# Keys and queries of a chunk made together as a 2 by 2 block product with seven products, the queries kept in DRAM

## The chip, the core and the metric

The kernel runs on one core of a Trainium2 chip. The metric is device time in microseconds (us). The kernel before took a median of 2603.17 us over three runs (2600.44 to 2604.17). Engines are named as the profile names them: PE (TensorE matmuls; PEld are its weight loads), DVE (VectorE), ACT (ScalarE), POOL (GpSimd) and SP (the queue that issues nearly all DMAs). All data is float32.

## The reference

Two layers run on x of shape 4 x 512 x 64 x 64 (four images, 512 channels, 4096 pixels). The first is self-attention over the pixels of an image:

```
q = wq @ xf + bq;  k = wk @ xf + bk;  v = wv @ xf + bv     # (4, 128, 4096)
attn = softmax(q^T k)                                      # (4, 4096, 4096)
x1 = wo @ (v attn^T) + bo + x
```

The second is an involution block: `out = relu(W1 x1)`, a 49-tap (7 x 7) weight per pixel and group made from `out`, the weighted sum of the 49 shifted copies of `out`, then `W3` and the residual x1.

## The kernel before

**Stages.** An image is worked on in 8 chunks of 512 pixels (`CH`). For each of the four images `b`, a **keys stage** (`keys_values`) makes all keys and values, then an **attention stage** (`attention`) goes through the 8 query chunks. In the keys stage the chunks come in the order 2, 3, ..., 7, 1, 0; a chunk gives `pk` (4 matmuls of 512 columns) for the keys, and `pv` (16 matmuls of 128 columns) for the values. ACT moves both out of PSUM. In the attention stage each of 32 steps of a chunk makes one score tile `pss` (keys by queries), its exponential `pt` on ACT, one matmul into `po`, and on DVE a running sum `pacc` of the `pt` tiles. At step 24 of a chunk `queries` makes the queries of the next chunk: four matmuls of 512 columns into `pq`, moved out by ACT. The queries of chunk 0 are made in the keys stage.

**Work beside it.** A finished chunk goes through `finish_block` (normalising, `pwo` and the residual on DVE at L565, `p` for W1) and its result is written to DRAM (`pix`), from where windows come back into a ring in SBUF. The involution runs on units of 4 image rows, 16 of them per image: DVE multiplies a piece of the ring by the tap weights (`prod`, L358), POOL adds the product to `acc` (L382, folded at L391), DVE transposes the sum (`turned`, L406), and `close_chunk` applies W3 (`py`, residual on DVE at L463). 49 taps make a unit; a "tap row" below is one tap of one unit.

**What sets the order.** The work of the involution and of the finishing is spread between the matmuls by hand: `chores()` is called after a few matmuls, and runs steps of the generators `finishing`, `closing` and `taps`. A planner holds a clock of PE's time (`pe`, advanced by `mm`) and the times at which DVE, POOL and the DMAs would be free (`takes`). A tap is only issued when DVE's planned backlog is at most 3.5 us (4.5 for the last image) and POOL's is at most `lag`. Behind this the tile layer puts each engine's instructions into an order of its own; an engine runs that order strictly. After the last attention stage a tail runs what is left of the involution. PSUM pools: `ps_s` (two banks, for `pk` and `pss`), `ps1` (single banks `po`, `acc`, and the tap weights), `ps` (two banks, the rest). The x tiles come from six buffers, the `pt` tiles from five.

Of the kernel before, what the change touches and what calls it, by code (L numbers as in the profile page):

```python
# [8 lines left out]
F32 = mybir.dt.float32  # L9
# [58 lines left out]

PE_COLUMN = 0.43 / 256
DVE_OP, POOL_OP = 0.7, 1.28  # L70
DVE_TAPS, POOL_TAPS = (0.16, 0.27), (0.19, 0.55)
ROW_US, X_US, PIX_US, LAND_US = 2.2, 3.8, 1.5, 3.0
HOP_US = 0.8
# [12 lines left out]
def fast_path(  # L86
# [22 lines left out]
    def pool(name, bufs, **kw):  # L109
# [35 lines left out]
    okr = const.tile([P, 1], F32, name="okr")  # L145


    turns = [
        scratch.tile([CH // P, P, P], F32, tag=f"turns{i}", name=f"turns{i}") for i in range(2)
    ]  # L150
# [13 lines left out]
    reds, sums_c = {}, {}  # L164
    written = {}
    landing = {}
    lag = 0.0
    low, load = 0, 0

    def until(us):  # L170
# [14 lines left out]
        nc.sync.dma_start(xs[b, c], x_r[b, :, :, c * CH : (c + 1) * CH])  # L185


    for cols in (slice(0, P), slice(P, O_WV)):
        nc.scalar.dma_start(wt[:, cols], wts[:, cols])
    nc.scalar.dma_start(vec, vecs)  # L190
    c0, c1 = KEYS[:2]
    xs = {(0, c0): xpool.tile([P, CT, CH], F32, tag="x", name=f"x_0_{c0}")}
    for t in range(CT):
        nc.sync.dma_start(xs[0, c0][:, t, :], x_r[0, :, t, c0 * CH : (c0 + 1) * CH])
    nc.sync.dma_start(wt[:, O_WV:O_WQ], wts[:, O_WV:O_WQ])
    load_x(0, c1)
    nc.sync.dma_start(wt[:, O_WQ:], wts[:, O_WQ:O_WR])
    nc.vector.memset(ones, 1.0)

    warm = ps.tile([P, P], F32, tag="mm", name="warm")  # L200
# [16 lines left out]
    def v1(i):  # L217
        return vec[:, i : i + 1]
# [89 lines left out]
    def involution():  # L308
        nonlocal low, due
        while True:  # L310
# [15 lines left out]
            for o, (x, dy, n) in enumerate(ops):  # L326
                if o and dy >= DYS[1][0] > ops[o - 1][1]:
                    low = base + UR
                    pump()
                    if tail and units:  # L330
                        early[units[0]] = weights(*units[0])
                rows = [(base + dy + t * 2) % RING for t in range(NT)]
                while base + dy + n + NT > load:
                    yield "wait"
                landed = max(landing[base + dy + i] for i in range(n + NT))
                while not tail and (
                    pe < max(begin, landed)
                    or free["dve"] > pe + (4.5 if b == B - 1 else 3.5)
                    or free["pool"] > pe + lag
                ):  # L340
                    yield "wait"
                free["pool"] = max(free["pool"], takes("dve", DVE_TAPS[0] + DVE_TAPS[1] * n))
                takes("pool", POOL_TAPS[0] + POOL_TAPS[1] * n)
                due -= n
                d0 = dy - DYS[dy >= DYS[1][0]][0]
                first = x == 0 and dy < DYS[1][0]
                prod, p0 = acc, d0
                if not first:
                    prod, p0 = prods.tile(
                        [P, NT, 4, P], F32, tag="prod", name=f"prod_{b}_{u}_{o}"  # L350
                    ), 0
                col = (x * K + dy) * G
                lines = ring[:, rows[0] : rows[0] + n, x, :]
                image = bass.AP(
                    tensor=lines.tensor, offset=lines.offset,
                    ap=[lines.ap[0], [(rows[1] - rows[0]) * K * P, NT], [K * P, n], [1, P]],
                )
                product = nc.vector.tensor_tensor(  # L358
                    prod[:, :, p0 : p0 + n, :].rearrange("p t d (g c) -> p t d g c", g=G),
                    image.rearrange("p t d (g c) -> p t d g c", g=G),  # L360
                    pw[:, :, col : col + n * G].unsqueeze(3)
                    .broadcast_to([P, NT, n * G, GC])
                    .rearrange("p t (d g) c -> p t d g c", d=n),
                    ALU.mult,
                )
                if not tail:
                    tc.keep_in_program_order(product)
                if first:
                    pass
                elif tail and o % 2:  # L370

                    begun = pa is not None
                    if not begun:
                        pa = ps1.tile([P, NT, P], F32, tag=("po", "acc")[u % 2], name=f"pa_{b}_{u}")
                    for t in range(NT):
                        for d in range(n):
                            mm(
                                pa[:, t, :], prod[:, t, d, :], ident,
                                not begun and t == d == 0, False,
                            )  # L380
                else:
                    nc.gpsimd.tensor_tensor(  # L382
                        acc[:, :, d0 : d0 + n, :], acc[:, :, d0 : d0 + n, :], prod[:, :, :n, :],
                        ALU.add,
                    )
                yield
# [85 lines left out]
            nc.sync.dma_start(out_r[b, :, :, c * CH + off : c * CH + off + n], xt)  # L472


    def keys_values(b):
        kt = kvpool.tile([P, N], F32, tag="k", name=f"k_{b}")
        vT = kvpool.tile([P, N // P, P], F32, tag="v", name=f"v_{b}")

        for i, c in enumerate(KEYS):
            for k in KEYS[i + 1 : i + 3]:  # L480
                if (b, k) not in xs:
                    load_x(b, k)
            if c == 0:

                q = queries(b, 0, 0, CH)
            if b < 2 and i == 4:
                for rows in (slice(0, PAD), slice(PAD + H, None)):
                    nc.sync.dma_start(pix[b][rows].rearrange("r w c -> w r c"), zero)
                for cols in (slice(0, PAD), slice(PAD + W, None)):
                    nc.sync.dma_start(pix[b][PAD : PAD + H, cols, :], zero[:H])  # L490
            xt = xs[b, c] if c < KEEP else xs.pop((b, c))
            pk = ps_s.tile([P, CH], F32, tag="s", name=f"pk_{b}_{c}")
            for t in range(CT):
                mm(pk, w_slice(O_WK, t), xt[:, t, :], t == 0, t == CT - 1)
                if t % 2:
                    chores()
            nc.scalar.activation(
                kt[:, c * CH : (c + 1) * CH], pk, AF.Identity, bias=v1(V_BK)
            )
            pv = ps1.tile([P, 4, P], F32, tag=("po", "acc")[i % 2], name=f"pv_{b}_{c}")  # L500
            for j in range(4):
                for t in range(CT):
                    mm(
                        pv[:, j, :], xt[:, t, j * P : (j + 1) * P], w_slice(O_WV, t),
                        t == 0, t == CT - 1,
                    )
                if j % 2:
                    chores()
            nc.scalar.copy(vT[:, 4 * c : 4 * c + 4, :], pv)
        return kt, vT, q  # L510

    def queries(b, c, off, n):
        xt = xs[b, c][:, :, off : off + n]
        pq = ps.tile([P, CH], F32, tag="mm", name=f"pq_{b}_{c}_{off}")[:, :n]
        for t in range(CT):
            mm(pq, w_slice(O_WQ, t), xt[:, t, :], t == 0, t == CT - 1)
        q = work2.tile([P, CH], F32, tag="q", name=f"q_{b}_{c}_{off}")[:, :n]
        nc.scalar.activation(q, pq, AF.Identity, bias=v1(V_BQ))
        return q


# [198 lines left out]

    taps = [involution()]
    for b in range(B):
        lag = POOL_LAG[0]
        kv = keys_values(b)
        lag = POOL_LAG[1]
        if b == 0:

            pb = ps.tile([P, CT], F32, tag="mm", name="pb")
# [429 lines left out]
```

## Time and profile before

| | us |
|---|---|
| median of three runs | 2603.17 |
| the profiled execution, its own time | 2601.34 |
| span of the profiled execution | 2599.4 |
| PE busy / DVE busy / POOL busy / ACT busy | 2583.8 / 1874.6 / 1831.2 / 835.9 |
| keys stage of the second image (first to last matmul of it) | 616.64 to 689.55 |
| start of the last sum of the `pt` tiles (L715) | 2530.3 |

The granted PE clock is 1.000. In the lists of groups, a line gives the source line, engine, operation, tiles, sizes and count, then the busy time and the mean length of one in ns, then idle time of the engine just before it with what ended it. A float32 matmul shows as two PE instructions, so 128 matmuls of `pk` are 256 instructions. The end of a matmul in the trace is modelled, so the distance from start to start is the better measure of what it costs. In the timeline a line has its start in us, its length, engine, line and operation, and in brackets the idle time before it.

### The profile page before, as it was taken

How to read it: one execution, taken by the hardware profiler on the slowest of the kernel's cores; microseconds unless marked ns; L12 is line 12 of the kernel's file. 1: busy time of each engine (PE TensorE's matmuls, PEld its weight loads, DVE VectorE, ACT ScalarE, POOL GpSimd, SP SyncE). 2: the span in 40 equal slices, each digit the busy share in tenths (PEclk: the TensorE clock that was granted, in tenths of full speed). 3: DMA queues.
4: the chain of work that ended last, by engine and by line, in shares of the span. 5: the costliest groups of instructions: out<-in, count | busy, mean ns of one | idle time of the engine just before them, and what ended most of it. 6: DMA issues, size and time to landing. Idle time of an engine off the chain costs nothing. (4 is left out here: it accounts for less than half of the span.)

```text
span 2599.4 us, 24518 instructions
## 1 busy us (share of the span) xinstructions
PE 2583.8 (99%) x7462; PEld 1242.4 (48%) x7462; DVE 1874.6 (72%) x2679; ACT 835.9 (32%) x1379; POOL 1831.2 (70%) x1202
## 2 busy tenths in 40 slices
PE   9999999999999999999999999999999999999998
PEld 7444444445544444444654444444464444444577
DVE  0347778877575787788676677788856677777888
ACT  1333333332233333333223333333323333333330
POOL 0006788877881788888885468887877577778986
PEclk9999999999999999999999999999999999999999
DMA  6033233445615343233651434434463432223243
GB/s 237 1 74 63 55 81 78 99 99 150 164 43 113 63 101 87 66 83 80 182 134 44 105 69 101 97 83 85 109 175 79 113 94 73 71 63 75 66 112 92
DMA packets 208797, 244.32 MB, mean 94 GB/s; under 512 B 109640, under 2 KB 128528, under 8 KB 208528
## 3 DMA queue, kind: packets, MB, share of 16 engines
q1 hardware_dynamic: 208224, 242.31, 38.7%
q8 instruction: 60, 0.98, 0.2%
q14 instruction: 81, 0.66, 0.1%
q10 hardware_dynamic: 432, 0.36, 0.0%
HBM read 193.57 MB, written 49.06 MB: 93 GB/s over the span
## 5 line engine op out<-in xcount | busy, mean ns | idle before, releaser
L382 POOL TENSOR_TENSOR acc<-acc,prod 128x768 f32<-128x768 f32 (+3 forms) x1066 | 1707.1, 1620 | 746.0 <-DVE prod L358 701.9
L222 PE MATMUL pss<-q,k 128*128 128x512 f32 (+1 forms) x2112 | 1055.7, 584 | 0.0
L222 PE MATMUL po<-pt,v 128*128 128x512 f32 (+1 forms) x2112 | 1047.2, 580 | 0.0
L681 ACT ACTIVATE pt<-pss 128x512 f32<-128x512 f32 x1024 | 611.3, 597 | 1242.5 <-PE pss L222 1158.4
L358 DVE TENSOR_TENSOR prod<-ring,pw 128x512 f32<-128x512 f32 (+3 forms) x1092 | 888.5, 849 | 47.2 <-POOL acc L382 44.2
L712 DVE TENSOR_TENSOR pacc<-pacc,pt 128x512 f32<-128x512 f32 x958 | 666.0, 695 | 236.9 <-ACT pt L681 209.5
L222 PEld LDWEIGHTS po<-pt,v 128*128 128x128 f32 x2112 | 398.8, 190 | 480.9 <-issue 460.4
L222 PEld LDWEIGHTS pss<-q,k 128*128 128x128 f32 x2112 | 391.5, 190 | 466.8 <-issue 462.0
L406 DVE STREAM_TRANSPOSE turned<-acc 128x256 f32<-128x256 f32 x48 | 21.4, 445 | 218.4 <-POOL acc L391 218.4
L222 PE MATMUL py<-accT,wt 128*128 128x512 f32 (+1 forms) x264 | 132.2, 584 | 4.1 <-DVE x L463 3.5
L222 PE MATMUL pwo<-on,wt 128*128 128x512 f32 (+1 forms) x264 | 128.5, 579 | 0.0
L391 POOL TENSOR_TENSOR acc<-acc 128x512 f32<-128x512 f32 x122 | 121.6, 997 | 9.6
L222 PEld LDWEIGHTS pv<-wt,x 128*128 128x128 f32 x1024 | 119.6, 192 | 15.3 <-issue 15.3
L463 DVE SCALAR_TENSOR_TENSOR x<-py,vec,x 128x512 f32<-128x512 f32 (+1 forms) x132 | 95.9, 727 | 38.3 <-PE py L222 38.0
L222 PE MATMUL pv<-wt,x 128*128 128x128 f32 x1024 | 120.2, 275 | 0.0
L222 PE MATMUL p<-x,wt 128*128 128x512 f32 (+1 forms) x264 | 119.3, 580 | 0.0
L222 PE MATMUL pk<-x,wt 128*128 128x512 f32 x256 | 117.7, 599 | 0.0
L592 ACT ACTIVATE x<-x,vec 128x512 f32<-128x512 f32 (+1 forms) x132 | 92.9, 706 | 74.9 <-PE p L222 58.1
L222 PE MATMUL pq<-x,wt 128*128 128x512 f32 (+1 forms) x264 | 115.3, 579 | 0.0
L565 DVE SCALAR_TENSOR_TENSOR x<-pwo,bo,x 128x512 f32<-128x512 f32 (+1 forms) x132 | 95.3, 728 | 21.2 <-PE pwo L222 19.9
L358 DVE TENSOR_TENSOR acc<-ring,pw 128x1024 f32<-128x1024 f32 (+1 forms) x84 | 78.7, 956 | 15.6 <-PE pw L222 15.6
L222 PEld LDWEIGHTS pq<-x,wt 128*128 128x128 f32 x264 | 50.1, 190 | 59.7 <-issue 56.4
(69 smaller groups left out, 727.5 us busy)
## 6 DMA issues: line engine op xcount, KB each, us to landing
x<-x_dram SPq DMA_DIRECT2D x55, 1024.0 KB, 5.5
ring<-pix SPq DMA_DIRECT2D x74, 448.0 KB, 7.0
ring<-pix SPq DMA_DIRECT2D x24, 1344.0 KB, 9.7
out_dram<-x SPq DMA_DIRECT2D x31, 1024.0 KB, 4.6
ring<-pix SPq DMA_DIRECT2D x24, 896.0 KB, 10.5
ring<-pix SPq DMA_DIRECT2D x30, 672.0 KB, 10.8
ring<-pix SPq DMA_DIRECT2D x6, 2240.0 KB, 19.6
pix<-o1t SPq DMA_DIRECT2D x192, 32.0 KB, 1.7
```

The source lines that it names most:

```text
L222: return nc.tensor.matmul(o, lhsT=lhsT, rhs=rhs, start=start, stop=stop)
L358: product = nc.vector.tensor_tensor(prod[:, :, p0 : p0 + n, :].rearrange("p t d (g c) -> p t d g c", g=G), image.rearrange("p t d (g c) -> ...
L382: nc.gpsimd.tensor_tensor(acc[:, :, d0 : d0 + n, :], acc[:, :, d0 : d0 + n, :], prod[:, :, :n, :], ALU.add,)
L391: nc.gpsimd.tensor_tensor(acc[:, :, :n, :], acc[:, :, :n, :], acc[:, :, n : 2 * n, :], ALU.add)
L406: nc.vector.transpose(blocks.rearrange("p (t k q) -> p t k q", t=NT, q=TB), acc[:, :, 0, :].rearrange("p t (k q) -> p t k q", q=TB),)
L463: nc.vector.scalar_tensor_tensor(xt[:, t, :], py, v1(V_S3 + t), xt[:, t, :], ALU.mult, ALU.add)
L565: nc.vector.scalar_tensor_tensor(xt[:, t, :], pw, bo[:, t : t + 1], xt[:, t, :], ALU.add, ALU.add)
L592: nc.scalar.activation(xt[:, t, :], xt[:, t, :], AF.Identity, bias=v1(V_B3 + t))
L681: nc.scalar.activation(pt, pss, AF.Exp)
L712: nc.vector.tensor_tensor(paccs[k], paccs[k], pt, ALU.add)
```

## The change

For a chunk, the key and query weights, and the chunk's x, are seen as 2 by 2 blocks: the input channels are cut into two halves of 256, the pixels into two halves of 256. Keys and queries of the chunk are eight block products; the change makes them from seven:

- **Weights.** Once, at the start, DVE makes sums and differences of weight halves (`mixed`, three tiles of 128 x 256, and one in place in `wt`).
- **Pixels.** `pixel_sums` makes four sums or differences of the chunk's x blocks, each 128 x 512, on DVE, in buffers of the `pt` pool; those of the next chunk are made during the present one.
- **Products.** Each of the seven (`m1` to `m7`, of which `m4` lands where `m6` was) is two matmuls of 256 columns. `m1`, `m2` share the PSUM bank `m12`, `m6`, `m7` (and later `m4`) the bank `m67`, `m5`, `m3` the bank `m53`. ACT copies `m1` out; DVE adds the others in seven additions of 128 x 256 with one operand in PSUM.
- **Queries.** A chunk's queries are therefore made in the keys stage. Those of chunks 1 to 7 are written to DRAM (`q_out`, 256 KB each); `queries` is now a DMA that reads them back. The four `pq` matmuls of a chunk in the attention stage and ACT's move of it are gone, and so are `pk` and its move.
- **Values.** `pv` has one PSUM bank instead of two in turn, and is cut into pieces between the products. For the first chunk of an image it comes ahead of the products.
- **Planner.** In the keys stage a tap is only issued when DVE's planned backlog is at most 1.5 us.
- **Start.** The value weights are loaded first, on ACT's queue; key and query weights follow the first x tiles on SP, ahead of the second chunk's x.

The core of the diff (planner constants, loads at the start and the removal of `pk` and `pq` included):

```diff
-    for cols in (slice(0, P), slice(P, O_WV)):
+    for cols in (slice(O_WV, O_WV + P), slice(O_WV + P, O_WQ)):
         nc.scalar.dma_start(wt[:, cols], wts[:, cols])
...
-    nc.sync.dma_start(wt[:, O_WV:O_WQ], wts[:, O_WV:O_WQ])
+    nc.sync.dma_start(wt[:, :O_WV], wts[:, :O_WV])
+    nc.sync.dma_start(wt[:, O_WQ:O_WO], wts[:, O_WQ:O_WO])
     load_x(0, c1)
...
-                    or free["dve"] > pe + (4.5 if b == B - 1 else 3.5)
+                    or free["dve"] > pe + (1.5 if making else 4.5 if b == B - 1 else 3.5)
...
+    def halves(b, c):
+        xt = xs[b, c]
+        return [[xt[:, 2 * k : 2 * k + 2, h * HF : (h + 1) * HF] for h in range(2)] for k in range(2)]
+    def pixel_sums(b, c):
+        (b11, b12), (b21, b22) = halves(b, c)
+        out = []
+        for n, (x0, x1) in enumerate(((b12, b11), (b22, 0), (b22, b12), (b21, 1))):
+            pt = ptpool.tile([P, CH], F32, tag="pt", name=f"sum_{b}_{c}_{n}")
+            pt = pt.rearrange("p (t n) -> p t n", t=2)
+            takes("dve", DVE_OP)
+            nc.vector.tensor_tensor(pt, x0, out[x1] if x1 in (0, 1) else x1, ALU.subtract)
+            out.append(pt)
+        return out
...
+        def product(o, w, rhs):
+            for t in range(2):
+                mm(o, w[:, t * P : (t + 1) * P], rhs[:, t, :], t == 0, t == 1)
...
-            pk = ps_s.tile([P, CH], F32, tag="s", name=f"pk_{b}_{c}")
-            for t in range(CT):
-                mm(pk, w_slice(O_WK, t), xt[:, t, :], t == 0, t == CT - 1)
...
+            product(m1, k0, b11)
+            nc.scalar.copy(left, m1)
+            product(m6, s2, t2)
+            product(m7, q10, t3)
+            add(right, m6, left)
+            add(q[:, :HF], m7, right)
+            product(m5, s1, t1)
+            add(q[:, HF:], m5, q[:, :HF], V_BQ)
+            add(right, m5, right)
+            if i + 1 < NCH:
+                sums = pixel_sums(b, KEYS[i + 1])
+            if i == 0:
+                chores()
+            for j in range(3):
+                if i:
+                    values(pv, xt, (j,))
+                    if j != 1:
+                        chores()
+            product(m2, k1, b21)
+            add(left, m2, left, V_BK)
+            product(m6, q1, t4)
+            add(q[:, :HF], m6, q[:, :HF], V_BQ)
+            product(m3, s4, b22)
+            add(right, m3, right, V_BK)
+            if c:
+                nc.sync.dma_start(q_out[c], q)
...
     def queries(b, c, off, n):
-        pq = ps.tile([P, CH], F32, tag="mm", name=f"pq_{b}_{c}_{off}")[:, :n]
-        for t in range(CT):
-            mm(pq, w_slice(O_WQ, t), xt[:, t, :], t == 0, t == CT - 1)
         q = work2.tile([P, CH], F32, tag="q", name=f"q_{b}_{c}_{off}")[:, :n]
-        nc.scalar.activation(q, pq, AF.Identity, bias=v1(V_BQ))
+        nc.sync.dma_start(q, q_out[c][:, off : off + n])
         return q
...
-        lag = POOL_LAG[0]
+        lag, making = POOL_LAG[0], True
         kv = keys_values(b)
-        lag = POOL_LAG[1]
+        lag, making = POOL_LAG[1], False
```

## The prediction

> **What bounds the kernel now.** I read the page first: which engine has no idle time, and whether that holds in every slice.
>
> ```profile
> PE 2583.8 (99%) x7462; PEld 1242.4 (48%) x7462; DVE 1874.6 (72%) x2679; ACT 835.9 (32%) x1379; POOL 1831.2 (70%) x1202
> PE   9999999999999999999999999999999999999998
> DVE  0347778877575787788676677788856677777888
> POOL 0006788877881788888885468887877577778986
> ```
>
> PE is the only engine at nine tenths in every slice; its clock is granted in full. But modelled ends make "busy" uncertain, so I checked in the timeline whether the matmuls follow each other without gaps, first in the keys stage of the second image.
>
> ```profile
> 642.38 3.60 PE L222 MATMUL pk<-x,wt 128*128 128x512 f32 x8
> 645.81 3.73 PE L222 MATMUL pv<-wt,x 128*128 128x128 f32 x32
> 649.38 1.88 PE L222 MATMUL p<-x,wt 128*128 128x512 f32 x4
> ```
>
> From start to start, 8 instructions of `pk` take 3.43 us, 0.429 us each; 32 of `pv` take 3.57 us. Nothing is lost between them. Then the busy time by stage, here the second image's keys stage and its attention stage (columns PE, PEld, DVE, ACT, POOL, each with a count; clock, DMA share, GB/s):
>
> ```profile
> 617.00:690.00 73.00, 73.00 (x368) 47.62 (x367) 37.72 (x44) 15.00 (x24) 58.21 (x32) 1.00 0.67 181
> 690.00:1261.00 571.00, 569.64 (x1407) 249.72 (x1406) 436.94 (x635) 192.86 (x317) 417.62 (x279) 1.00 0.39 91
> ```
>
> So the time is PE's own work, in both stages; a matmul removed is time gained, as long as the others keep PE fed. DVE is half idle in the keys stage (37.7 of 73 us) and 77% busy in attention.
>
> **What a 256-column matmul costs.** The products are half as wide. The tail has such matmuls with new weights each time:
>
> ```profile
> 2542.10 1.03 PE L222 MATMUL pwo<-on,wt 128*128 128x256 f32 x4
> ...
> 2542.96 2.84 PE L222 MATMUL pa<-ident,prod 128*128 128x128 f32 x24
> ```
>
> Four instructions in 0.86 us: 0.215 each, half of 0.429. **The Trainium skill**, "TensorE: Matmul & The Clock Gate", section "Back-to-back issue gap", gives a gap of N/2.4 + 2.5 ns, and says that weight loads also count when N is small. The trace fits: 0.429 is about two such gaps at 512, 0.215 two at 256, and a weight load is 190 ns, so it just hides under 215. I go by the trace's row.
>
> **The change, part by part** (sums against the profiled execution: 2601.34 us, span 2599.4; the median of three, 2603.17, is 1.8 higher).
>
> *PE.* Removed: `pk` and `pq`, 4 + 4 matmuls or 16 instructions per chunk: 32 x 16 x 0.429 = 219.6 us. Added: 14 matmuls of 256 columns, 28 instructions: 32 x 28 x 0.215 = 192.6 us. **Saved: 27 us.** The `pv` work is the same.
>
> *Where it lies.* A keys stage grows by 8 x (6.02 - 3.43) = 20.7 us, less 3.4 for chunk 0's `pq`; an attention stage loses 7 x 3.43 = 24 us.
>
> *DVE.* These rows give the prices:
>
> ```profile
> L712 DVE TENSOR_TENSOR pacc<-pacc,pt 128x512 f32<-128x512 f32 x958 | 666.0, 695 | 236.9 <-ACT pt L681 209.5 <-DVE rls L549 0.2
> L358 DVE TENSOR_TENSOR prod<-ring,pw 128x256 f32<-128x256 f32 x140 | 57.6, 412 | 9.0 <-POOL acc L382 8.6 <-DMA ring<-pix 0.4
> L463 DVE SCALAR_TENSOR_TENSOR x<-py,vec,x 128x256 f32<-128x256 f32 x8 | 3.8, 482 | 4.3 <-PE py L222 4.3
> ```
>
> Per chunk: 4 pixel sums x 0.695 + 3 additions x 0.412 + 4 with a bias x 0.482 = 5.95 us; 190 us in all, plus four weight sums (1.6). None is PE's time by itself. In the timeline consecutive DVE operations start closer than they are long (612.03, 612.63, 613.23: 0.60 apart at 0.69 us), so in a row I count 0.60, 0.33 and 0.39.
>
> *ACT* loses about 32 x 2 x 0.687 and gains 32 copies of 128x256 (0.370 by `accT`): 32 us less, off the path, hence nothing.
>
> *DMA and SP.* 28 writes and 29 reads of queries (14.5 MB beside 244). The nearest row, `accT` with 256 KB, lands in 2.8 us. In the changed program's order each read stands where its buffer comes free, a chunk (about 65 us) ahead of its use: hidden; if the cover went, PE would wait at a chunk's first score. A store waits for DVE's last query addition, and x loads queue behind it on SP; they wait for an x buffer that PE frees later anyway. Zero.
>
> *The wait added: PE now waits for DVE in the keys stage.* PE's second use of `m53` (`m3`) needs four DVE results after `m5`. In the changed order DVE does, after `m5`: a pixel sum, the first key addition, a sum, the first query addition, a sum, two additions with `m5`: 0.2 (PE to DVE as with `py`) + 3 x 0.60 + 2 x 0.33 + 0.39 + 0.41 = 3.5 us. PE meanwhile has 12 `pv` matmuls (2.7), `m2` and the second use of `m6` (0.86 each): 4.4 us. So the first image's chunks run without a stall. The second place in the skill is "PSUM — Partial Sum Buffer", section "Engine vs sequencer instructions": DVE's queue is strict FIFO, so whatever stands ahead of an addition delays it. The trace agrees:
>
> ```profile
> 672.73 0.45 DVE L406 STREAM_TRANSPOSE turned<-acc 128x256 f32<-128x256 f32 x1 [5.15 <-POOL acc L391]
> 673.10 0.71 DVE L463 SCALAR_TENSOR_TENSOR x<-py,vec,x 128x512 f32<-128x512 f32 x1
> ```
>
> The `py` of that addition was done at about 669.5; it sat behind `turned`, which sat 5.15 us for POOL (218 us over 48 of them). Before, nobody waited for that. I walked the second image's keys stage in the changed order, with these distances and POOL's 2.36 / 1.82 us per tap of four / three rows. Two places stall.
> - First chunk (its `m1` at 0): `pv` stands ahead of the products here, so `m5` ends only at 7.1, and `m6`'s second use is due at 8.4 behind `m2` and a bit of the next `pv`. DVE can make the second sum of the next chunk only when `m5` has freed its buffer: 7.3 to 7.9; then the previous image's normalising (`on`) to 8.5, the key addition to 8.9, a sum to 9.5, the query addition to 10.0. PE waits 1.6 us.
> - Fifth chunk (`m5` at its end at 3.5): `turned` is next on DVE but one. The last of three taps of the chunk before left DVE 0.9 us into this chunk; POOL, one behind, adds three at 1.82 and folds (2.0), done at 6.6. DVE's chain then runs from 7.2 to 10, still in time for `m3` (10.4: two `p` pairs and `pw` lengthen PE's part). But the order sets a transpose (0.6) and three taps of 1.13 ahead of `m2`'s addition: done at 14.4, where the sixth chunk's `m1` was due at 12.2. PE waits some 2.3 us.
>
> The orders of images 2 to 4 are alike: **3 x 4 = 12 us.** Bounds: 0 if POOL is done earlier, 24 if every tap-bearing chunk (24) loses 1 us.
>
> *Start.* Before, the first `pk` lost about 1 us to loads. Now the weight sums need the query weights, 256 KB later (1.1 us at the first slice's 237 GB/s), then two DVE operations, and a pixel sum of chunk 2 waits for its x ahead of the first addition. I take **+3**, bounds 1 and 6.
>
> *Taps and tail.* Counting tap rows in the two orders: images 2 to 4's keys stages issue 74 instead of 100, but the attention stages catch up; after the last `pt` sum 156 remain instead of 150. The tail took 2599.4 - 2530.3 = 69 us for 150: **+2**, bounds 0 and 4. DVE is then 88% full in attention instead of 83% (19 of `pacc`, 30 of taps, 8 of finishing in 65 us); the planner still holds its backlog to 3.5 us there. Zero, up to 6.
>
> *Sum.* 2601.3 - 27 + 12 + 3 + 2 = 2591; **I predict 2591 us**, -0.4% (a measurement of this kernel tells about 0.2%, 5 us, from no change).
>
> **Rivals.**
> A. *All additions stay hidden.* For it: slack of 0.9 us per chunk, and a keys stage in which DVE has about 80 us of work by lengths (8 x 5.95, 23 of taps, 9 of finishing) in PE's 87 (8 x 9.6 and 10 of other matmuls). Against: DVE's wait for `turned`. 2601.3 - 27 + 3 + 2 = 2579.
> B. *Each tap-bearing chunk loses about 1 us* because taps stand ahead of additions that PE wants. 24 x 1 + 5 = 29 against 27: 2603, no change. For: DVE is filled to 90% by lengths there; against: taps are held to a planned 1.5 us.
> C. *The DVE chain is longer than PE's cover in every chunk*: slower. If each of the seven links from `m5` to `m3` took 0.35 us more (a handover between PE and DVE on a shared bank, which no row of the trace shows), the chain would be 6.0 against 4.4: 32 x 1.6 = 51, so 2601 - 27 + 51 + 5 = 2630. It decides from 0.7 us of stall per chunk. Against: `py` to L463 shows 0.2 us.
> D. *The seven products don't stream at 0.215.* If a weight load showed through by 0.03, 896 x 0.03 = 27 us: no gain, 2603 or above. Against: the 256-column row above. Counted with B.
>
> **Chances.** Forecast (2585 to 2597) 0.43; A 0.27; B and D 0.17; C 0.13. The range takes in A and most of B: 2575 to 2606. Faster by over 0.2% 0.70, within 0.17, slower 0.13.
>
> **What would show it.** Two product instructions should start 0.215 us apart; PE idle ahead of `m` tiles, released by DVE, should be about 12 us in three keys stages and sit in the first and the fifth to sixth chunk; the first image's keys stage should have none after its first chunk; each attention chunk should be 3.4 us shorter; the tail about 2 us longer. PE gaps in attention released by ACT `pt`, or PE idle in every chunk of the first image, would make the forecast wrong.

## The result, and the profile after

The changed kernel takes 2649.08 us, median of 4 runs (2646.38 to 2651.43), against 2602.39 (2600.44 to 2604.17) before: ratio 1.0181, 95% interval 1.0169 to 1.0193. The forecast was 2591. The profiled execution took 2651.43 us with a span of 2649.6.

The page of the kernel after, in the lines that were shown of before: busy time by engine, then the 40 slices.

```profile
PE 2588.5 (98%) x7876; PEld 1322.8 (50%) x7876; DVE 2068.2 (78%) x3035; ACT 804.2 (30%) x1346; POOL 1832.2 (69%) x1198
...
PE   9999999999999999999999999999999999999998
...
DVE  5447788888776788788888678878877877888887
...
POOL 0006788884684688888477378888837777888886
```

PE still shows nine tenths everywhere, although the kernel is slower: a tenth of a 65 us slice is 6.5 us, so short gaps vanish in this view, and halving the clock makes PE look busy. The stages of the second image show more (columns as before; the stage borders are this kernel's own):

```profile
616.44:713.36 96.92, 90.42 (x507) 75.94 (x507) 78.75 (x126) 11.21 (x21) 45.97 (x26) 0.98 0.54 147
713.36:1265.99 552.63, 542.53 (x1304) 233.61 (x1303) 438.59 (x635) 186.30 (x307) 425.09 (x280) 0.99 0.40 92
```

PE is idle for 6.5 us of the keys stage and 10.1 us of attention, where it had 0 and 1.4, and the mean granted clock is below 1. The window 690 to 1261 that the forecast took for the attention stage of before ends 12 us inside the third image's keys stage, which begins at 1249.2. Between the true borders DVE had 430 us of work in 559.7 us before and has 438 us in 551.9 after: the stage is only 8 us shorter, where 24 were forecast, and DVE is fuller in it. Who is waited for, in the list of PE's waits (total, times, longest):

```profile
PE pl L227 <- DVE blocks L624: 11.8, 7, 1.9
PE pw L227 <- DVE prod L363: 10.1, 8, 2.6
PE m L227 <- DVE q L562: 8.6, 8, 1.2
PE m L227 <- DVE k L564: 7.1, 3, 2.4
PE py L227 <- DVE rls L633: 6.4, 4, 2.5
```

Two of the five are the additions that the change brought (`m`). The other three are waits of matmuls that the kernel before had as well. There only `pw` waited for the same DVE work, 0.7 us, and `py` for DVE's addition of the `py` before it (L463), 3.5 us.

To split the whole span I took each distance from one matmul's start to the next against its unhindered distance (0.429 us at 512 columns, 0.2155 at 256, 0.1115 at 128). An excess with PE idle is a wait; an excess while the granted clock stands at one half is put down to the clock. The split is good to about 2 us: by the number of instructions the matmuls of 512, 256 and 128 columns need 22.4 us less after the change, where the first row has 20.3.

| us of the span | before | after | forecast of the difference |
|---|---|---|---|
| unhindered matmuls | 2539.2 | 2518.9 | -25 (tail included) |
| waits in keys stages | 0 | 25.3 | +12 |
| waits in attention | 5.4 | 30.7 | 0 |
| waits in the tail | 4.2 | 4.9 | |
| half clock | 0 | 14.5 | |
| rest (start, ends, small) | 50.6 | 55.3 | +3 (start) |
| span | 2599.4 | 2649.6 | -10 |

**One keys stall in full.** In the timeline of the fifth and sixth chunk of image 2, first DVE, then PE (start, duration, engine, line, operation, and in brackets the idle time before it with its releaser):

```profile
671.96 0.45 DVE L411 STREAM_TRANSPOSE turned<-acc 128x256 f32<-128x256 f32 x1 [5.75 <-POOL acc L396]
...
675.51 1.18 DVE L363 TENSOR_TENSOR acc<-ring,pw 128x1024 f32<-128x1024 f32 x1
676.62 2.34 DVE L363 TENSOR_TENSOR prod<-ring,pw 128x1024 f32<-128x1024 f32 x2
678.88 0.47 DVE L564 SCALAR_TENSOR_TENSOR k<-m,vec,k 128x256 f32<-128x256 f32 x1
```

```profile
679.40 1.27 PE L227 MATMUL m<-x,wt 128*128 128x256 f32 x4 [2.36 <-DVE k L564]
680.46 1.91 PE L227 MATMUL m<-sum,mixed 128*128 128x256 f32 x4
682.17 1.78 PE L227 MATMUL m<-sum,wt 128*128 128x256 f32 x4
```

DVE stood 5.75 us for POOL; then a transpose and three taps ran ahead of the addition `k` that frees the next chunk's bank. PE waited 2.36 us, and then a group of four instructions took 1.7 us (680.46 to 682.17) where it takes 0.86 (639.97 to 640.84 in the same stage). The stall is the one forecast (2.3 us); the slow matmuls behind it are not.

**One attention stall in full**, in the first image, DVE and then PE:

```profile
477.30 2.94 DVE L363 TENSOR_TENSOR prod<-ring,pw 128x1024 f32<-128x1024 f32 x3
480.15 0.69 DVE L799 TENSOR_TENSOR sums<-pacc,pt 128x512 f32<-128x512 f32 x1
480.88 0.71 DVE L624 TRANSPOSE_TENSOR_REDUCE blocks<-sums 128x16 f32<-128x512 f32 x1
```

```profile
481.64 0.40 PE L227 MATMUL pl<-blocks,quads 128*128 128x16 f32 x2 [1.92 <-DVE blocks L624]
481.89 1.67 PE L227 MATMUL pss<-q,k 128*128 128x512 f32 x2
483.35 1.91 PE L227 MATMUL po<-pt,v 128*128 128x512 f32 x2
```

Three taps of 1024 columns stand ahead of `sums` and `blocks` on DVE; `pl`, in PE's order, holds up all scores behind it. Nothing of the seven products (Strassen's scheme) runs here.

### The profile page after: what moved, and what is told of

Same layout as the page of the kernel before. It is cut to its first block, busy times and chain, and to the rows that moved or that the text cites. A ratio compares the mean times of both kernels' runs of the same rounds, so it can differ in the third digit from the quotient of the medians.

```text
span 2649.6 us, 25977 instructions
## 1 busy us (share of the span) xinstructions
PE 2588.5 (98%) x7876; PEld 1322.8 (50%) x7876; DVE 2068.2 (78%) x3035; ACT 804.2 (30%) x1346; POOL 1832.2 (69%) x1198
## 3 DMA queue, kind: packets, MB, share of 16 engines
q1 hardware_dynamic: 216608, 256.99, 39.7%
## 4 chain that ended last, share of the span: by engine, by line
PE 50%; POOL 21%; DVE 18%; issue 10%; ACT 0%; POOLq 0%; DVEq 0%; ACTq 0%
POOL acc L387 18%; PE pss L227 17%; PE po L227 17%; DVE prod L363 7%; PE m L227 5%; DVE pacc L796 4%; POOL acc L396 3%; PE pwo L227 2%; PE pv L227 2%; PE p L227 2%; PE py L227 2%; DVE sum L492 2%; DVE acc L363 2%; PE pw L227 1%; DVE x L468 1%
## 5 line engine op out<-in xcount | busy, mean ns | idle before, releaser
L363 DVE TENSOR_TENSOR prod<-ring,pw 128x512 f32<-128x512 f32 (+3 forms) x1092 | 898.0, 850 | 74.1 <-POOL acc L387 72.8
L227 PEld LDWEIGHTS pv<-wt,x 128*128 128x128 f32 x1024 | 126.1, 192 | 11.2 <-issue 7.4
L227 PE MATMUL pv<-wt,x 128*128 128x128 f32 x1024 | 127.6, 275 | 0.0
L596 ACT COPY v<-pv 128x512 f32<-128x512 f32 x32 | 18.8, 587 | 241.5 <-PE pv L227 241.5
L227 PEld LDWEIGHTS py<-accT,wt 128*128 128x128 f32 x264 | 47.5, 191 | 66.4 <-issue 39.7
L227 PEld LDWEIGHTS p<-x,wt 128*128 128x128 f32 x264 | 49.6, 190 | 56.4 <-issue 50.7
```

Of the source, the lines that this page charges most:

```text
L227: return nc.tensor.matmul(o, lhsT=lhsT, rhs=rhs, start=start, stop=stop)
L363: product = nc.vector.tensor_tensor(prod[:, :, p0 : p0 + n, :].rearrange("p t d (g c) -> p t d g c", g=G), image.rearrange("p t d (g c) -> ...
```

## The experiments

**Theory.** DVE executes in order and had little room; the change gives it 190 us more to do and takes 24 us of PE's work per image from the stage in which DVE does most of its own. So it runs some us further behind, and PE's few matmuls with a short way from DVE (`pl`, `py`, `pw`, the products) wait. **Rivals**: only the handover of the additions in the keys stages costs (K); the shortened attention by itself (S) or the load by itself (L); and that steps which stood well by their places were displaced, so that any other spacing would cost as much (P).

All times are medians; the ratio is to the kernel before on the same chip, with its 95% interval. "Keys", "attention" and "half" are the waits and the clock loss of the split above, in us; DVE is its busy share (overlaps counted once) in the second image's attention stage, where I worked it out. e17 has two runs, every other kernel four or more.

| kernel | us | ratio | keys | attention | half | DVE |
|---|---|---|---|---|---|---|
| before | 2601 to 2602 | 1 | 0 | 5.4 | 0 | 0.768 |
| after | 2649.1 | 1.0181 [1.0169, 1.0193] | 25.3 | 30.7 | 14.5 | 0.792 |
| e1_move_q | 2628.9 | 1.0104 [1.0087, 1.0121] | 0 | 20.0 | 9.6 | 0.779 |
| e16_move_q_half | 2605.1 | 1.0015 [1.0008, 1.0022] | 0 | 1.5 | 0 | 0.649 |
| e6_load_only | 2608.4 | 1.0028 [1.0018, 1.0038] | 2.2 | 9.2 | 1.8 | 0.79 |
| e20_load_placed | 2668.0 | 1.0252 [1.0235, 1.0269] | 6.0 | 45.8 | 22.6 | 0.802 |
| e15_more_dve | 2605.4 | 1.0016 [1.0009, 1.0022] | 0 | 5.6 | 1.4 | 0.771 |
| e19_more_dve_placed | 2630.3 | 1.0108 [1.0091, 1.0125] | 0 | 24.3 | 6.5 | 0.836 |
| e4_half_pacc | 2620.9 | 1.0077 [1.0061, 1.0094] | 23.0 | 7.2 | 8.4 | 0.670 |
| e17_half_no_taps | 2637.2 | 1.0137 [1.0117, 1.0157] | 7.3 | 14.0 | 6.8 | |
| e7_later | 2626.5 | 1.0098 [1.0082, 1.0115] | 3.0 | 39.6 | 5.0 | 0.793 |
| e8_wide | 2659.1 | 1.0222 [1.0205, 1.0239] | 19.9 | 42.3 | 20.8 | |
| e10_wide_early_turn | 2688.0 | 1.0336 [1.0319, 1.0353] | 23.3 | 58.4 | 30.5 | |
| e11_quiet | 2670.5 | 1.0263 [1.0245, 1.0280] | 17.6 | 53.2 | 23.2 | |
| e3_pool_sums | 2640.9 | 1.0153 [1.0136, 1.0170] | 16.0 | 31.9 | 17.3 | |
| e9_wide_before | 2629.2 | 1.0109 [1.0092, 1.0126] | 7.0 | 19.3 | 1.5 | 0.755 |
| e13_before_later | 2613.9 | 1.0050 [1.0033, 1.0066] | 0 | 14.8 | 2.7 | |
| e12_quiet_before | 2635.8 | 1.0130 [1.0113, 1.0146] | 0 | 29.9 | 8.5 | |
| e14_move_q_later | 2638.2 | 1.0138 [1.0121, 1.0155] | 0.3 | 31.8 | 6.7 | |
| e18_first_image | 2601.5 | 1.0000 [0.9992, 1.0009] | 1.8 | 9.7 | 0 | |

### Which part of the change costs

**e1_move_q**, from before:

```diff
-            if c == 0:
-                q = queries(b, 0, 0, CH)
+            q = make_queries(b, c)          # the plain pq, in the keys stage
+            if c:
+                nc.sync.dma_start(q_out[c], q)
...
     def queries(b, c, off, n):
+        nc.sync.dma_start(q, q_out[c][:, off : off + n])
```

> The kernel before with one part of the change alone: the queries of every chunk are made in the keys stage, still with the plain four matmuls of pq, stored to DRAM and read back for their attention chunk. No Strassen, no pixel sums, no additions; the matmul work is that of before. Three theories. S (shorter attention: the same DVE and POOL work falls on an attention stage that is 24 us shorter, and PE waits for DVE there): about 30 us slower than before, 2625 to 2640, with PE gaps behind DVE in attention as after the change. L (load: the pixel sums and additions take DVE from the taps of the keys stage, and the taps pushed out fill DVE in attention): 2600 to 2607, since no DVE work is added and the keys stages even get 116 tap rows instead of 100. K (handover: the loss comes from PE waiting for the additions in the keys stage, all else follows from it): 2600 to 2604.

Measured 28 us slower. The keys stages have no wait at all; attention waits rise from 5.4 to 20 us and 9.6 us go to the clock. PE's waits:

```profile
PE pl L226 <- DVE blocks L549: 7.4, 4, 1.9
PE pwo L226 <- DVE x L574: 5.3, 3, 3.6
PE pw L226 <- DVE prod L362: 3.7, 6, 0.9
```

So moving matmuls out of attention costs 28 us with not one DVE operation added, against the 58 by which the forecast was missed, and L and K fell as sole causes. The move also gives PE and DVE another order of instructions, so by itself this run doesn't tell S from P.

**e16_move_q_half**, from e1:

```diff
             elif j < nj - 1:
-                nc.vector.tensor_tensor(paccs[k], paccs[k], pt, ALU.add)
+                if j % 2:
+                    nc.vector.tensor_tensor(paccs[k], paccs[k], pt, ALU.add)
```

> The kernel before with the plain queries moved to the keys stage (2629), and every second addition of the row sums left out in attention (half of each row sum is missing from the result): DVE gets 9 of 65 us back in the shortened stage. Load theory: the cost of the move goes but for a tail some 3 to 5 us longer: 2602 to 2612. Places theory: 2615 to 2635.

Measured 2605.1, attention waits 1.5 us. The planner still counts the additions left out, so the order is that of e1: PE's instructions stand in the same order up to 2483 us but for one swap, and on DVE, row sums aside, some twenty single ones have changed places. With the places all but held, the cost is gone: where DVE has room, the shorter stage costs nothing.

**e4_half_pacc**, the same edit on the kernel after (again with PE's order held but for one swap, up to 2505 us):

> The kernel after with every second addition of the row sums left out in attention (so half of each row sum is missing from the result): some 14 to 15 DVE operations of 0.6 us less per attention chunk, about 9 of 65 us; the keys stages are unchanged. S and L alike (DVE is too full in attention): the PE waits of the attention stages and the clock windows behind them go, 31 + 8 us of the 2649: 2605 to 2618, with the keys stages still 97 us long. K: 2640 to 2649.

Measured 2620.9, a little above the range of S and L: 7.2 us of waits in attention and 8.4 of half clock were left. In its list of PE's waits `pl` and `py` no longer lead; the products do, as large as they were:

```profile
PE m L227 <- DVE q L562: 8.1, 8, 1.3
PE m L227 <- DVE k L564: 7.1, 3, 2.4
```

Attention waits fell from 30.7 to 7.2 us, those of the keys stages from 25.3 to 23.0. There are two losses, then, and they are separate.

**e17_half_no_taps**, from e4:

```diff
-                    or free["dve"] > pe + (1.5 if making else 4.5 if b == B - 1 else 3.5)
+                    or free["dve"] > pe + (-99 if making else 4.5 if b == B - 1 else 3.5)
```

> The kernel after with half of the row sums left out, as in e4, and no tap started in the keys stages; 74 rows per image go to attention or to the tail, which grows from 162 to 264 rows, some 45 us. What counts is the length of the keys stages of images 2 to 4 (97.3 us in e4, of which 7 are waits). If taps ahead of the additions make PE wait there: the stalls of the fifth and sixth chunk go, some 3.5 us each with their half-clock windows, and a stage takes 90 to 93 us. If the handover itself costs: 96 to 98 us.

The keys stages of images 2 to 4 took 87.6, 87.5 and 94.8 us (97.3, 97.2, 97.8 in e4), their waits 2.4, 1.5 and 3.4 us instead of 6.9, 6.9 and 8.0. The seven products and eleven DVE operations are all still there, so the handover itself is nearly free, as in the first image (1.7 us of waits). What makes PE wait is the tap work of the stage: taps and `turned` ahead of the additions, and POOL's operations, which also stretch the pixel sums (last section). The run takes both away and doesn't part them. The taps now fall into attention and the tail: attention waits rise from 7.2 to 14.0 us. The total is worse above all because of the longer tail (from the start of the last sum of the `pt` tiles 114 us, 77 in e4).

**e6_load_only** and **e15_more_dve** were to add DVE load to the kernel before, in the keys stages and in attention:

```diff
+    # e6, per chunk of keys_values: 4 x and 7 x
+            nc.vector.tensor_tensor(pt, xt[:, 0:2, HF:], xt[:, 0:2, :HF], ALU.subtract)
+                nc.vector.tensor_tensor(o, wt[:, O_WK : O_WK + HF], wt[:, O_WK : O_WK + HF], ALU.add)
+    # e15, in attention, at every sixth j
+                nc.vector.tensor_tensor(idle, wt[:, :CH], wt[:, :CH], ALU.add)
```

> The kernel before with the DVE load of the change alone: in the keys stages, four 128x512 subtractions and seven 128x256 additions per chunk of which nobody reads the result; keys and queries are made as before. The keys stages of images 2 to 4 then issue 49 tap rows instead of 100. S: about 2602, at most 2607, since attention has its old length. L: 2625 to 2645, PE gaps behind DVE in attention and half-clock windows after them, none in the keys stages. K: about 2602.

> The kernel before with five more additions of 128x512 on DVE per attention chunk, of which nobody reads the result: 3 of 69 us, so that DVE is as full in attention as it is after the change (83% to 87 or 88%). Load theory: 2618 to 2640, PE gaps behind DVE and half-clock windows as after the change. Places theory (P): the taps shift a little, but distances are kept: 2602 to 2612.

Measured 2608.4 and 2605.4, but neither tests its theory as meant: operations that read only constants were moved forward when the program was built, and the trace has all 224 additions of e6 before 160 us and all 159 of e15 before 142 us. Only e6's 112 subtractions (112 us in all; 0.68 us the median one) stayed in place. Both show something else. In e6 the planner did push 51 tap rows per image out of the keys stages, DVE is 0.79 full in attention, as after the change, and yet PE waits only 9.2 us there. And in e15 the planner's bookings deal PE's order anew, about as far from that of before as e1's, for 4 us.

**e20_load_placed** and **e19_more_dve_placed** repeat them with data of the moment:

```diff
-                nc.vector.tensor_tensor(o, wt[:, O_WK : O_WK + HF], wt[:, O_WK : O_WK + HF], ALU.add)
+                nc.vector.tensor_tensor(o, xt[:, 0, :HF], xt[:, 0, :HF], ALU.add)
...
-                nc.vector.tensor_tensor(idle, wt[:, :CH], wt[:, :CH], ALU.add)     # ahead of the score
+                nc.vector.tensor_tensor(idle, pt, pt, ALU.add)     # behind the matmul into po
```

> The kernel before with the DVE load of the change alone, now in its place: per chunk of the keys stages four 128x512 subtractions and seven 128x256 additions that read that chunk's x; nobody reads the results. Images 2 to 4 start 49 tap rows in the keys stages instead of 100 and so 55 more in attention, 7 per chunk, which is 1.9 us of DVE. Load theory: 2612 to 2635, with waits in attention and few in the keys stages. If only the handover of the additions costs: 2600 to 2607.

> The kernel before with five more 128x512 additions on DVE per attention chunk, now reading the chunk's own exponentials, so that they run in it: 3 of 69 us, and nobody reads the result. Load theory: PE waits behind DVE rise by 15 to 30 us with half-clock windows after them: 2615 to 2640. Places theory: 2601 to 2612.

e19 took 2630.3: operations nobody waits for make the kernel 29 us slower. The load was larger than meant, though: both inputs of `idle` lie in SBUF, and its 159 operations took up to 2.7 us, 197 us in all, some 6 us per chunk in place of 3 (see the last section), so DVE is fuller there (0.836) than after the change.

e20 took 2668.0, more than expected. Its waits are 45.8 us in attention and only 6.0 in the keys stages, and they are not those of the kernel after:

```profile
PE pw L224 <- DVE prod L360: 29.9, 14, 4.4
PE pss L224 <- ACT pt L714: 7.5, 7, 2.5
```

It is not a pure test of the keys stage: of its 56 additions per image, 14 ran up to 130 us early, inside attention. And the load is too large: its additions read SBUF twice and took 166 us, those of the change, with an operand in PSUM, 101.

**e20 against e6** is the cleanest test of load, though it wasn't planned as one. Leaving out the added operations, PE (7462 instructions), POOL and ACT run exactly the same order in both, and DVE the same but for four swaps of neighbours. The taps pushed out are therefore the same, and so are all places; what differs is whether the additions run where they were written. e20 is 60 us slower, and PE falls behind in three stretches of 170 to 200 us, from the first of an image's additions to some 30 us behind the last. In the 440 us of attention between two stretches it keeps its distance to e6 within 2 us. So load on DVE does cost PE time with the order held, close to where it runs. The taps pushed out, which e6 has too, cost 8 us at most.

### Do places or distances explain it

**e7_later**, from after (and **e13_before_later**, **e14_move_q_later**, the same on before and on e1):

```diff
-        yield from pause(free["dve"], 3)
+        yield from pause(free["dve"], 5)
...
-            yield from pause(spreads, 5)
+            yield from pause(spreads, 6)
```

> The kernel after with more distance between a chunk's DVE operations and the matmuls that read them: five steps instead of three ahead of the row-sum product pl, six instead of five ahead of the output projection. DVE's work is the same. If the waits in attention are DVE's backlog of a few us ahead of a short-latency consumer (S and L), the distance covers those of pl: 2630 to 2642. If DVE were short of throughput as such, the waits would only move and the time stay at 2645 to 2652. K: 2649.

> The kernel before with the two distances that made the kernel after 23 us faster (pl five steps after its row sum, the projection six after its spread). It asks whether the 28 us of the moved queries come from the shorter attention stage (S) or from a displacement of steps that stood well by their places in the kernel before (P: any other spacing costs some 25 us, as the wider distances did here). S: 2598 to 2606. P: 2612 to 2632.

> The same two distances on the kernel before with the plain queries moved to the keys stage (2629 without them). S: the shorter stage keeps its cost: 2618 to 2632. P: the places fall anew, and with luck the cost is gone: 2600 to 2614.

The kernel after gained 22.6 us, more than expected, yet not in attention, whose waits rose to 39.6: it gained in the keys stages (3.0 us of waits with 69 tap rows in place of 74) and in the clock, as the waits became shorter. The kernel before lost 13 us, e1 lost 9. So the distances are no remedy; they deal the collisions anew (PE's order in e7 is far from that of after). For e13 the range of P held, at its edge; e14 lies above both ranges.

**e8_wide**, **e10_wide_early_turn** and **e9_wide_before** widen every distance at which a trace had shown a wait (e9 on before; e10 without the second edit):

```diff
-    ptpool = pool("pt", 5)
+    ptpool = pool("pt", 7)
...
-        yield from until(done + 2.0)
+        yield from until(done + 5.0)
...
-                for _ in range(3):          # ahead of py
+                for _ in range(5):
...
-        yield from pause(free["dve"], 3)    # ahead of pl
+        yield from pause(free["dve"], 5)
...
-                for _ in range(t % 2 if late else 1 + (t != 1)):
+                for _ in range(t % 2 if late else 2):
...
-            yield from pause(spreads, 5)
+            yield from pause(spreads, 7)
```

> The kernel after with distance at every place where a trace showed PE or DVE waiting in attention: pl five steps after its row sum (three before), the projection seven after its spread (five), two steps between its four products, py five steps after its transposed sum (three), the transpose of a finished unit 5 us after POOL's planned end (2), seven buffers of exponentials (five). DVE, POOL and PE do the same work. S, now the theory: the loss is latency, not throughput, so the PE waits and half-clock windows of attention go: 2585 to 2605, below the kernel before if the keys stages' waits shrink too, as they did with five and six steps. Rival T (DVE and POOL lack throughput in the shorter stage): the waits move elsewhere and the time stays at 2620 to 2630.

> The same as e8_wide but for the transpose of a finished unit, which keeps its place 2 us after POOL's planned end. In the run with five and six steps DVE stood up to 6.9 us at that transpose for POOL, with the additions of the row sums behind it. If that stop is the main one left: 2600 to 2620, 10 us or more above e8_wide. If the distances to PE's consumers alone do it: within 4 us of e8_wide.

> The kernel before with the distances of e8_wide. S: it has only some 5 us of PE waits in attention to lose: 2596 to 2603. If the distances were worth as much here as after the change (20 us or more), the loss would not be the change's: 2580 or below.

The levels expected fell in all three; only that e10 lies over 10 us above e8 held. e8 is 10 us slower than after, e10 39, and e9 28 slower than before. My reading that the loss was only latency was wrong: more distance moved `py` to where the two banks that it shares with `pl` were held by `rls` (18.0 us of waits in e8, 39.7 in e10, 14.2 in e9; 6.4 after). Taking `turned` 3 us later is worth 29 us between e10 and e8. Of the 7.0 us of waits in e9's keys stages, 6.5 are for loads of x, not for DVE.

**e11_quiet** and **e12_quiet_before** replace distances by rules:

```diff
-                    or free["dve"] > pe + (1.5 if making else 4.5 if b == B - 1 else 3.5)
+                    or free["dve"] > pe + (1.5 if making else 1.5 if quiet else 4.5 if b == B - 1 else 3.5)
...
+            while quiet and not tail:       # ahead of each py
+                yield
```

> The kernel after with two rules instead of distances: from two steps ahead of a chunk's row sum until its spread is used, taps may run DVE only 1.5 us ahead of PE (3.5 otherwise), and no py product is started, since py takes the buffer that DVE must have read for rls. The collision theory (P: a step of short latency meets three taps ahead of it on DVE, or the buffer of another such step): the waits of pl and of py for rls go, 2610 to 2630. If the waits go by DVE's total work: 2645 to 2655.

> The same two rules on the kernel before, which shows few such collisions: P and S both 2596 to 2606; a rise by over 10 us would mean that the rules themselves displace other steps.

e11 fell outside both of its ranges, 21 us slower than after, and e12 is 35 us slower than before: the rules displace other steps. `pl` now waited 13.7 and 14.0 us. In e12's timeline, DVE:

```profile
758.74 0.45 DVE L406 STREAM_TRANSPOSE turned<-acc 128x256 f32<-128x256 f32 x1 [8.13 <-POOL acc L391]
...
764.33 2.35 DVE L358 TENSOR_TENSOR prod<-ring,pw 128x1024 f32<-128x1024 f32 x2
766.59 0.68 DVE L722 TENSOR_TENSOR sums<-pacc,pt 128x512 f32<-128x512 f32 x1
767.31 0.71 DVE L543 TRANSPOSE_TENSOR_REDUCE blocks<-sums 128x16 f32<-128x512 f32 x1
```

DVE had stood 8.1 us for POOL's last fold, and then had its backlog to clear ahead of `sums`. No limit on taps in the planner sees this stop. There are 43 to 48 such stops in each of the ten runs in which I counted them, 190 to 242 us in all.

**e3_pool_sums**, from after:

```diff
-            takes("dve", DVE_OP)
-            nc.vector.tensor_tensor(pt, x0, out[x1] if x1 in (0, 1) else x1, ALU.subtract)
+            takes("pool", POOL_OP)
+            nc.gpsimd.tensor_tensor(pt, x0, out[x1] if x1 in (0, 1) else x1, ALU.subtract)
```

> The kernel after with the pixel sums on GpSimd instead of VectorE, 2.8 us less per chunk of the keys stages on DVE. If DVE's load in the keys stages were the cause (L), attention would get its taps back and the time would fall to 2615 to 2635. S: attention stays as it is, and the sums now stand behind POOL's taps, with PE waiting for them: 2650 to 2680.

Measured 2640.9, between the two: keys waits fell from 25.3 to 16.0 us (10.3 us of what is left is for POOL's sums), attention stayed at 31.9.

**e18_first_image** keeps the scheme in the first image, whose keys stage has no taps, and the functions of before for the others (`s3` in a fourth tile instead of over the query weights):

```diff
-        kv = keys_values(b)
+        kv = (plain_keys_values if b else keys_values)(b)
...
+        return (plain_queries if b else stored_queries)(b, c, off, n)
```

> The scheme in the first image alone, whose keys stage has no taps and had 1.7 us of waits; images 2 to 4 are those of the kernel before. 8 chunks x 0.84 = 6.7 us less for PE, 1 to 2 us at the start, and the first image's attention stage is 24 us shorter with DVE fuller: it gained 4 us of waits and half clock after the change. Load theory: 2597 to 2604, no gain that a measurement tells. If the scheme pays where DVE is free: 2594 to 2597.

Measured 2601.5, no difference that can be told. Unhindered matmuls take 6.3 us less, 2532.9, and the waits rise by 6.3 (from 9.5 to 15.8), most in the first attention stage (5.2 against 1.8). Even there waits for DVE give the gain back. No version of the scheme that I ran beats the kernel before.

## Why the prediction was wrong

The bridge in the profiled execution, from the forecast's sum 2591.3: keys waits +13.3 (25.3 for 12), attention waits +25.3, half clock +14.5, unhindered matmuls +4.7 (-20.3 for -25), rest and tail waits +5.4 with the +3 of the start taken off, +2.4: together 60.2, or 2651.5 for 2651.43.

- **PE's saving, and 0.215 per product: right.** In the first image's keys stage PE's work grew by 17.3 us, as forecast, and groups of four product instructions start 0.86 to 0.87 apart. Rival D is out. (The gap that the forecast took from the skill is the page's figure for a single isolated matmul; the trace's row carried the forecast.) By the number of instructions PE saves 26.6 us and pays 4.2 for more taps added up by PE in the last image: 396 instructions of 128 columns instead of 358, 38 x 0.1115. The other 2 us of the 4.7 are the uncertainty of the split.
- **The wait added: places right, size too small.** The stalls stand in the first and the fifth to sixth chunk of images 2 to 4, released by DVE, with one more in the seventh chunk of image 3 (0.99); 2.36 us at `m1` was forecast at 2.3. But in the first chunk `pl` of the image before waits as well (1.4 to 1.7 us), and in the fifth the second use of `m6` (1.06), so 7 to 9 us a stage instead of 4. A term was mis-sized too: pixel sums at 0.695 us took 115.1 us for 128, 0.90 each, because 37 of them ran against POOL.
- **The step that failed** is the one that costed the fuller DVE in attention: "the planner still holds its backlog to 3.5 us there. Zero, up to 6." In its place attention has 25.3 us more of waits, and of the half clock 11.3 us lie there. The sentence took the planner's account for DVE's queue. That account limits taps, but it knows neither DVE's stops for POOL (73 us at `prod`, 190 at `turned`) nor what a matmul with a distance of three steps can bear. With the order held, DVE's work decides: 9 of 65 us less, and the attention waits go from 20.0 to 1.5 us (e1 to e16) and from 30.7 to 7.2 (after to e4); more work in the same places, and they go from 9.2 to 45.8 (e6 to e20). How full DVE is decides nothing by itself: at 0.79 e6 waits 9.2 us and the kernel after 30.7. (The forecast's 83% and 88% were too high as well; the trace has 0.768 and 0.792.)
- **The rule cited from the Trainium skill, "PSUM — Partial Sum Buffer", "Engine vs sequencer instructions" (DVE is strict FIFO), decided the case.** I applied it in the keys stage, where the additions are new, and not in attention, where `pl`, `py` and `pw` had hung on the same queue all along, with 4.2 us to show for it (`py` 3.5, `pw` 0.7).
- **Half clock: no term at all.** It nearly doubles the price of a wait of about 2 us.
- **Start, tail, DMA, SP: inside their bounds.** The first image's keys stage is 18.6 us longer, so only some 1.3 us beside the 17.3 of PE's work, for +3; it waited 1.7 us. From the start of the last sum of the `pt` tiles the tail takes 72.8 us instead of 69.0, for +2. No wait of PE on a stored query appears.
- **Rivals.** B's size for the keys stages (24) came true, by another distribution; C had the sign, but its mechanism is refuted by the first image and by e17.

**What stays open** is why the waits of attention came with this change: because the shorter stage leaves DVE less room, or because the new order put DVE's work in worse places. Load is shown to matter within an order, by e16, e4 and e20. But new orders at the load of before cost anything from 4 us (e15) and 13 (e13) to 28 (e9) and 35 (e12), e9 with DVE at 0.755, and the 28 of e1 lie among them; those of the kernel after gave -23 to +39. So the strong form of P, that any other spacing would cost as much, is wrong, and a weaker one, that the change drew a bad order, is not excluded. The shares can't be separated by spacings that also deal everything else anew. A `turned` put well behind POOL's end, which e8 against e10 points to, was not tried further.

## What to carry to other kernels

Price DVE's added work by the stage in which its in-order queue meets PE's shortest dependency, and ask of a shortened stage whether the other engines' work still fits: here PE's saving in attention came through only where DVE was given room. A view in which PE shows nine tenths everywhere doesn't say how much room the others have: look at each matmul with a short way from DVE, what stands ahead of its producer, and where that engine stops for a third one. In a schedule of hand-set distances a change that moves nothing but time can cost some 30 us of 2600, so test the parts (work moved, load added, load removed) before the whole is judged, and look in the trace whether an added load runs where it was written. Compare the order of instructions of two runs before their times: only where the order is the same does the difference belong to the edit alone.

## What the runs showed of the hardware

**VectorE against GpSimd.** Pixel sums read both inputs from SBUF. In the first chunk of the second image's keys stage, DVE and then POOL:

```profile
617.75 1.52 DVE L492 TENSOR_TENSOR sum<-x 128x512 f32<-128x512 f32 x1
619.20 0.68 DVE L799 TENSOR_TENSOR sums<-pacc,pt 128x512 f32<-128x512 f32 x1
619.80 1.15 DVE L492 TENSOR_TENSOR sum<-x,sum 128x512 f32<-128x512 f32 x1
...
626.18 0.67 DVE L492 TENSOR_TENSOR sum<-x 128x512 f32<-128x512 f32 x1
```

```profile
614.99 7.09 POOL L387 TENSOR_TENSOR acc<-acc,prod 128x512 f32<-128x512 f32 x5
```

While POOL runs (to 622.1) a sum takes 1.52 and 1.15 us, afterwards 0.67; `sums`, which has one input in PSUM, takes 0.68 in between. The two stretched sums stand ahead of `blocks` and are 1.3 us longer than alone; `pl` waited 1.37 us behind them (621.63). In the whole run the 37 sums that met a POOL operation already running took 1.44 us on average and up to 2.51, the other 91 took 0.68. The additions read PSUM, and none of the 64 `k<-m,k` took over 0.426 us. The Trainium skill, "SBUF — State Buffer", section "Who interferes with whom", says that a DVE instruction with two SBUF inputs contends with a GpSimd instruction that reads SBUF, and that the pair of ports they share is an exclusive lock: whoever comes second stands until the other is done. The trace agrees, and shows it sharply: whatever was left of the POOL operation it met (0.12 to 1.96 us), each of the 37 sums ended 0.55 to 0.58 us after that operation's end. I had not looked there for the price of the sums.

**The clock.** After PE gaps of about 2 us the granted clock drops to a half for 3.4 us (482.3 to 485.7 behind the attention stall shown above), or for twice that, which costs 1.5 to 1.7 us for each 3.4. Over the traces of before, after and the eighteen experiments, without the first 300 us, such a window began in the gap or within 3.5 us behind it for 13 of 138 gaps of 1.0 to 1.6 us, 19 of 45 of 1.6 to 2.0 us, 41 of 56 of 2.0 to 3.0 us, and all 26 of 3 us and more. The Trainium skill, "TensorE: Matmul & The Clock Gate", section "Why this matters for your kernels", warns of idle gaps above about 3 us; here gaps of 2 us mostly suffice, and the measurement decides.
